# A hybrid layer of selective scan, attention and spectral filters: tokens laid over the partitions in blocks of 128 neighbours

## The chip, the cores and the metric

The kernel runs on one core of a Trainium2 chip. The metric is device time in microseconds (us) of a whole execution, as the median of several runs. Below, TensorE is called PE, VectorE DVE, ScalarE ACT, GpSimd POOL, and SyncE, which issues the transfers, SP, as the profile calls them.

## The reference

The input is 4 images (batches) of 48 x 48 positions, that is 2304 tokens, with 128 channels in float32. Two layers follow each other. Cut to what matters here:

```
# layer 0: selective scan (256 inner channels, 16 states, 4 directions)
xz = gn(x) @ in_proj_w.T;  xin, z = split(xz)
xc = silu(depthwise_conv3x3(xin));  y = sum of 4 directional scans of xc
y  = layernorm(y) * silu(z);        x = x + y @ out_proj_w.T
# layer 1: attention without projections, then STU
t = tokens(x)
n = ln(t);  t = t + softmax(n @ n.T) @ n          # 2304 x 2304 a batch
u = ln(t)
t = t + STU(u)   # causal convolutions of u with 16 filters, and a 3-tap
                 # autoregression; four weightings over 1, 1/2, 1/4, 1/8 of the tokens
```

All arithmetic of the kernel is float32.

## The kernel before

A batch goes through four pieces of work. The **prologue** normalizes the image, projects it and convolves it. The **scans** run the four directions in chunks of 384 tokens: ACT makes exponentials, DVE runs the recurrences (L461), POOL and PE sum over the states. The **epilogue** normalizes the sum of the scans, gates it, projects it to 128 channels and adds it to the residual. **Attention** follows, and its `tail` ends it. Then comes **STU**. Work of different batches is laid over one another: STU of batch b runs beside the scans of batch b+1, on PE above all, and the prologue of batch b+1 is handed out, task by task, between the steps of the epilogue and of the attention of batch b. After the last batch, STU runs alone.

The schedule is written out by hand: each engine executes its instructions in the order in which the program issues them, and the generators (`next(at)`, `parts.pop(0)()`) set that order. So an engine that waits holds up all that was issued to it later. DMAs are issued by SP alone in this part of the kernel, in order too, and SP itself waits where a transfer needs another one to have landed.

The 2304 tokens are cut into five pieces: `PIECES = [4, 4, 4, 4, 2]`, in blocks of 128 tokens, so four pieces J of 512 tokens and a last one of 256. The residual of the batch is held in SBUF as `T`, 128 partitions x 18 columns of 128 channels; piece J takes the columns 4J to 4J + n. Which token lies where is told by one function, `tokens(x, J)`, used for the load of `T` (L613) and for the store of the attention's result to the DRAM tensor `td` (L874):

```python
return x[512 * J:512 * J + P * n].rearrange("(p j) c -> p j c", j=n)
```

Partition p thus holds n neighbouring tokens, 2 KB in one stretch for n = 4. STU wants the tokens split into four phases, token modulo four, and with n = 4 the columns of `T` are those phases. The last piece has n = 2, and for it alone `tail` reads `td` back into a tile `tu` in four phases (L880).

The epilogue works channel-major: `yf` (the tensor `ya`) and `zr` hold channels on the partitions and tokens along the free axis. Its output must be token-major, so they are the stationary operand of the projection `op` (L654), and `sq` is that of the variance `var` (L639); the 128 tokens of column j are taken with a stride of n:

```python
nc.tensor.matmul(var[:, 4 * J + j:4 * J + j + 1], sq[J][:, 0, j:P * n:n], dmean[:, 0:1], ...)
nc.tensor.matmul(p[:, i, f], x[h][:, lo:lo + P * n - j0 - f:n], w[:, h], ...)
```

The stages of the epilogue are staggered over the pieces. One step (slot) issues, oldest piece first: the normalization for attention (`norm`), `add(J,2)` (L663, L665: DVE adds the projection, scaled by `rd`, to `T`), `project(J,2)` with `add(J,0)`, then for the next piece `project(J,0)` with `variance(J)` (its `rd`: DVE L642, POOL L643), for the next `gate` (DVE L633, POOL L634), then `center` (DVE L626, ACT L627) and `means` (PE L619). The two PSUM buffers of `op` alternate, so a projection waits for the `add` of the one two before it. Between these stages stand the prologue's tasks (transposes L195 with the copy L199 and the statistics L200).

Attention takes the pieces of queries in the order 0, 4, 1, 2, 3, each in 18 slots: scores `s` (L718), exponential `e` (ACT, L720), values `o` (L711). The tail of a finished piece is handed out one step a slot during the next piece: transposes `otr`, `add` to `T` (L871, L872), the store `td`, the normalization (`normed`: `ln_su` L149, L151, ACT `usq` L152, L154, POOL L156, L158), transposes `utr` (L890), copy `uT` (L893) and store `ud` (L895). The tail of piece 3 has no slots left and is issued at a stretch; after it come the first instructions of the next stage: STU's `prime` (L970) and its loads `tt<-fd` (L953) on SP, and the scans of the next batch.

Of the kernel before, what the change touches and what calls it, by code (L numbers as in the profile page):

```python
# [8 lines left out]
F32 = mybir.dt.float32  # L9
# [6 lines left out]
P = 128  # L16
B, H, W, C = 4, 48, 48, 128
# [38 lines left out]
def hybrid_kernel(ctx: ExitStack, tc: tile.TileContext, a: dict, out: bass.AP):  # L56
# [3 lines left out]
    nc = tc.nc  # L60
# [51 lines left out]
    dmean = wp.tile([P, P], F32, name="dmean")  # L112
# [20 lines left out]
    td = res.tile([L, C], F32, name="td")  # L133
# [6 lines left out]
    def tokens(x, J):  # L140

        n = PIECES[J]
        return x[512 * J:512 * J + P * n].rearrange("(p j) c -> p j c", j=n)

    def normed(x, d, eps, small, sq, name):

# [448 lines left out]
    def epilogue(b, T, xn, xnT, tmp, pool, ps):  # L595

        yf = [t.rearrange("p h w -> p (h w)") for t in yaccs.pop(b)]
        zr, mu, o, sq, rd, lns, pt = {}, {}, {}, {}, {}, {}, {}
        var = ps.one.tile([P, 512], F32, tag="var", name=f"var{b}")

        def at(J):
            return slice(512 * J, 512 * J + P * PIECES[J])

        def load_z(J):
            n = P * PIECES[J]  # L610
            zr[J] = tmp.tile([P, NH, 512], F32, tag=f"zr{J}", name=f"zr{b}_{J}")
            nc.sync.dma_start(zr[J][:, :, :n], zs[:, :, at(J)].rearrange("h p t -> p h t"))
            nc.sync.dma_start(T[:, 4 * J:4 * J + PIECES[J]], tokens(a["x"][b], J))  # L613

        def means(J):
            n = P * PIECES[J]
            mu[J] = ps.two.tile([P, 512], F32, tag="mu", name=f"mu{b}_{J}")
            for h in range(NH):
                nc.tensor.matmul(mu[J][:, :n], dmean, yf[h][:, at(J)], start=(h == 0), stop=(h == NH - 1))  # L619

        def center(J):
            n = P * PIECES[J]
            sq[J] = tmp.tile([P, NH, 512], F32, tag=f"esq{J % 3}", name=f"sq{b}_{J}")
            for h in range(NH):
                v = yf[h][:, at(J)]
                nc.vector.tensor_tensor(v, v, mu[J][:, :n], ALU.subtract)  # L626
                nc.scalar.activation(sq[J][:, h, :n], v, AF.Square)  # L627

        def gate(J):
            n = P * PIECES[J]  # L630
            for h in range(NH):
                v = yf[h][:, at(J)]
                nc.vector.tensor_tensor(v, v, zr[J][:, h, :n], ALU.mult)  # L633
            nc.gpsimd.tensor_tensor(sq[J][:, 0, :n], sq[J][:, 0, :n], sq[J][:, 1, :n], ALU.add)  # L634

        def variance(J):
            n = PIECES[J]
            for j in range(n):
                nc.tensor.matmul(var[:, 4 * J + j:4 * J + j + 1], sq[J][:, 0, j:P * n:n], dmean[:, 0:1],  # L639
                                 start=True, stop=True)  # L640
            rd[J] = tmp.tile([P, 4], F32, tag=f"rd{J}", name=f"rd{b}_{J}")[:, :n]
            nc.vector.tensor_scalar_add(rd[J], var[:, 4 * J:4 * J + n], 1e-5)  # L642
            nc.gpsimd.tensor_tensor(rd[J], rd[J], mhalf[:, :n], ALU.pow)  # L643

        def project(J, j0):
            n = PIECES[J]
            if j0 >= n:
                return
            o[J, j0] = p = ps.two.tile([P, 2, 2, C], F32, tag="o", name=f"op{b}_{J}_{j0}")
            for f in range(2):  # L650
                for i, (x, w) in enumerate(((yf, owg), ([zr[J][:, h] for h in range(NH)], owb))):
                    lo = 512 * J * (i == 0) + j0 + f
                    for h in range(NH):
                        nc.tensor.matmul(p[:, i, f], x[h][:, lo:lo + P * n - j0 - f:n], w[:, h],  # L654
                                         start=(h == 0), stop=(h == NH - 1))

        def add(J, j0):
            if j0 >= PIECES[J]:
                return
            p = o.pop((J, j0))  # L660
            for f in range(2):
                t = T[:, 4 * J + j0 + f]
                nc.vector.scalar_tensor_tensor(t, p[:, 0, f], rd[J][:, j0 + f:j0 + f + 1], t, ALU.mult, ALU.add)  # L663
            t = T[:, 4 * J + j0:4 * J + j0 + 2]
            nc.vector.tensor_tensor(t, t, p[:, 1], ALU.add)  # L665

        def norm(J):
            if J not in lns:
                n = PIECES[J]
                sq = pool.two.tile([P, 4, C], F32, tag="ln_sq", name=f"asq{b}_{J}")[:, :n]  # L670
                lns[J] = normed(T[:, 4 * J:4 * J + n], xn[:, 4 * J:4 * J + n], 1e-5, pool.two, sq, f"a{b}_{J}")
            next(lns[J], None)

        def turned(J):
            pt[J] = ps.two.tile([P, 512], F32, tag="tr", name=f"xtr{b}_{J}")
            for j in range(PIECES[J]):
                nc.tensor.transpose(pt[J][:, j * P:(j + 1) * P], xn[:, 4 * J + j], ident)

        def kept(J):
            nc.scalar.copy(xnT[:, at(J)], pt.pop(J)[:, :P * PIECES[J]])  # L680
            nc.gpsimd.memset(xn[:, 4 * J:4 * J + PIECES[J], C - 1:], 1.0)

        for J in range(len(PIECES)):
            load_z(J)
        stages = [means, center, gate, lambda J: (project(J, 0), variance(J)), lambda J: (project(J, 2), add(J, 0)),
                  lambda J: add(J, 2), norm, norm, norm, turned, kept]
        for slot in range(len(PIECES) + len(stages) - 1):
            for s, stage in reversed(list(enumerate(stages))):
                if 0 <= slot - s < len(PIECES):
                    stage(slot - s)  # L690
                    yield slot - s if stage is kept else None
# [158 lines left out]
    def tail(b, J, T, po, pool, ps):  # L850


        u, sums = us[b]
        n, k = PIECES[J], KP[J]
        T = T[:, 4 * J:4 * J + n]
        oT = pool.two.tile([P, 512], F32, tag="oT", name=f"oT{b}_{J}")
        nc.vector.tensor_copy(oT[:, :P * n], po[:, :P * n])
        yield
        p = ps.two.tile([P, 4, C], F32, tag="tr", name=f"otr{b}_{J}")[:, :n]
        for j in range(n):  # L860
            nc.tensor.transpose(p[:, j], oT[:, j * P:(j + 1) * P], ident)
        yield
        r, s = [pool.two.tile([P, 4], F32, tag=f"den{i}", name=f"den{i}_{b}_{J}")[:, :n] for i in range(2)]
        nc.vector.tensor_copy(r, p[:, :, C - 1])
        nc.vector.reciprocal(r, r)
        nc.vector.tensor_reduce(s, p[:, :, :C - 1], AX.X, ALU.add)
        nc.vector.tensor_tensor(s, s, r, ALU.mult)
        yield
        for j in range(n):
            t = T[:, j, :C - 1]  # L870
            nc.vector.scalar_tensor_tensor(t, p[:, j, :C - 1], r[:, j:j + 1], t, ALU.mult, ALU.add)  # L871
        nc.vector.tensor_tensor(T[:, :, C - 1], T[:, :, C - 1], s, ALU.subtract)  # L872
        yield
        nc.sync.dma_start(tokens(td, J), T)  # L874
        x = T
        if n < 4:

            yield
            x = pool.one.tile([P, 4, C], F32, tag="tu", name=f"tu{b}")
            nc.sync.dma_start(x[:k], td[512 * J:].rearrange("(p j) c -> p j c", j=4))  # L880
            for i in range(3):
                yield
        sq = pool.one.tile([P, 4, C], F32, tag="sq", name=f"usq{b}_{J}")
        for _ in normed(x[:k], u[:k, J], 1e-5, pool.two, sq, f"u{b}_{J}"):
            yield
        nc.vector.tensor_tensor(sums[:k, J], u[:k, J, 0:2], u[:k, J, 2:4], ALU.add)
        yield
        p = ps.two.tile([P, 512], F32, tag="tr", name=f"utr{b}_{J}")[:, :4 * k]
        for j in range(4):
            nc.tensor.transpose(p[:, j * k:(j + 1) * k], u[:k, J, j], ident[:k, :k])  # L890
        yield
        uT = pool.two.tile([P, 4 * P], F32, tag="uT", name=f"uT{b}_{J}")[:, :4 * k]
        nc.scalar.copy(uT, p)  # L893
        yield
        nc.sync.dma_start(ud[:, :, 1 + P * J:1 + P * J + k], uT.rearrange("c (j p) -> c j p", j=4))  # L895
# [255 lines left out]
    for b in range(B):  # L1151
# [14 lines left out]
        T = back.one.tile([P, NT, C], F32, tag="T", name=f"T{b}")  # L1166
# [93 lines left out]
```

## Time and profile before

| | |
|---|---|
| median of 3 runs | 6137.34 us (6124.15 to 6143.45) |
| the profiled execution, its own time | 6131.63 us |
| its span, first to last instruction | 6129.9 us |
| PE busy | 5042.3 us, 82% |
| DVE busy | 4264.0 us, 70% |
| POOL busy | 3630.6 us, 59% |
| ACT busy | 3258.1 us, 53% |
| DMA | 1062.79 MB, 173 GB/s over the span |
| PE L654 `op` (two halves, x288 each) | 79.1 and 76.2 us busy |
| PE L639 `var`, x144 | 32.9 us busy |
| SP L613 T<-in_x, SP L874 td<-T | 20 issues each |
| SP L880 tu<-td | 4 issues |

A busy time is summed over the span; the share is of the span. PE overlaps one instruction's end with the next one's start, so for a series the distance of two starts says more than the length of one. A matmul of the program appears as two PE instructions. The epilogue and attention of the four batches lie at about 1104 to 1394, 2466 to 2757, 3832 to 4121 and 5202 to 5438 us of the span. "Granted clock" is the share of full speed at which PE was allowed to run.

### The profile page before, as it was taken

To read this page: it belongs to the slowest core of one execution; us is meant where nothing else is said; L and a number is where in the kernel's file an instruction comes from. 1 tells how busy PE (TensorE), PEld (TensorE's weight loads), DVE (VectorE), ACT (ScalarE), POOL (GpSimd) and SP (SyncE) were. 2 spreads that over 40 slices of the span, in tenths; PEclk is the share of its full clock that TensorE was granted. 3 is DMA by queue.
4 is the path that set the end of the run, shared out by engine and by line. 5 is a ranking of instruction groups with operands and counts; after the bars stand their busy time and mean duration, and the time that the engine had idled before them with its cause. 6 is when DMAs were issued, how large, how long until landed. Compare 5 with 4: busy or idle time off the path is not lost.

```text
span 6129.9 us, 76036 instructions
## 1 busy us (share of the span) xinstructions
PE 5042.3 (82%) x24850; PEld 3316.1 (54%) x24850; DVE 4264.0 (70%) x4926; ACT 3258.1 (53%) x6909; POOL 3630.6 (59%) x1823
## 2 busy tenths in 40 slices
PE   3555555797889988788889988888889998889999
PEld 1111111445556667545556666535556666558889
DVE  6999999458888998458888898448889998210000
ACT  2666666246666665247666665247666665232111
POOL 1988889307788888207788888108778887100000
PEclk6777777799999999899999999889999999899999
DMA  3445444117767777117767777027777776035546
GB/s 109 157 147 165 156 157 159 33 65 205 215 209 244 234 248 250 38 65 223 210 216 238 234 245 247 30 79 220 210 222 236 233 251 228 7 87 156 159 141 208
DMA packets 734954, 1062.79 MB, mean 173 GB/s; under 512 B 158272, under 2 KB 543424, under 8 KB 734528
## 3 DMA queue, kind: packets, MB, share of 16 engines
q1 hardware_dynamic: 728736, 1054.63, 54.6%
q10 hardware_dynamic: 5824, 3.30, 0.3%
q8 instruction: 199, 3.26, 0.2%
q14 instruction: 195, 1.60, 0.1%
HBM read 939.60 MB, written 117.98 MB: 173 GB/s over the span
## 4 chain that ended last, share of the span: by engine, by line
PE 43%; DVE 25%; DMA 11%; ACT 10%; SPq 5%; issue 4%; POOL 2%; ACTq 0%; DVEq 0%; POOLq 0%
PE cx L992 13%; DVE s L461 12%; PE cy L992 6%; DVE s L451 6%; DMA rep<-dtdud 4%; PE s L718 4%; PE y L478 3%; PE o L711 3%; ACT dA L458 3%; SPq L430 3%; DMA bc<-xdd 3%; PE pr L1055 2%; DMA tt<-fd 2%; PE pr L1051 2%; PE op L654 2%
## 5 line engine op out<-in xcount | busy, mean ns | idle before, releaser
L461 DVE TENSOR_TENSOR_SCAN s<-dA,s 128x385 f32<-128x385 f32 x3072 | 2735.4, 942 | 496.5 <-ACT dA L458 494.2
L470 POOL TENSOR_TENSOR s<-s,bc 128x1536 f32<-128x1536 f32 x768 | 2440.1, 3178 | 171.7 <-DVE s L461 95.0
L458 ACT ACTIVATE dA<-rep,A 128x384 f32<-128x384 f32 x3072 | 1747.2, 584 | 504.0 <-DVE s L461 471.2
L451 POOL TENSOR_TENSOR s<-rep,bc 128x1536 f32<-128x1536 f32 x288 | 993.4, 3449 | 90.6 <-DMA bc<-xdd 90.6
L478 PE MATMUL y<-s,csum 128*32 128x384 f32 x6144 | 723.9, 546 | 239.7 <-DVE ya L484 154.6
L992 PE MATMUL cx<-tt,u 128*128 128x254 f32 (+7 forms) x3840 | 830.8, 361 | 83.6 <-DMA tt<-fd 49.2
L992 PE MATMUL cx<-tt,us 128*128 128x254 f32 (+7 forms) x3840 | 809.5, 353 | 52.3 <-ACT U L1012 24.9
L451 DVE TENSOR_TENSOR s<-rep,B 128x1536 f32<-128x1536 f32 x480 | 830.4, 1730 | 14.2 <-ACT B L443 14.2
L992 PEld LDWEIGHTS cx<-tt,u 128*128 128x128 f32 x3840 | 653.5, 197 | 279.9 <-issue 132.9
L992 PE MATMUL cy<-tt,u 128*128 128x252 f32 (+5 forms) x3840 | 787.1, 348 | 0.0
L992 PEld LDWEIGHTS cx<-tt,us 128*128 128x128 f32 x3840 | 641.2, 191 | 240.3 <-issue 82.8
L992 PEld LDWEIGHTS cy<-tt,u 128*128 128x128 f32 x3840 | 639.8, 190 | 146.2 <-issue 85.9
L1079 DVE TENSOR_TENSOR res<-res,ot 126x512 f32<-126x512 f32 (+1 forms) x20 | 13.4, 671 | 686.5 <-PE ot L1073 686.1
L478 PEld LDWEIGHTS y<-s,csum 128*32 128x32 f32 x6144 | 128.3, 112 | 589.8 <-issue 375.5
L469 POOL COPY carry<-s 128x4 f32<-128x4 f32 x640 | 121.6, 190 | 535.2 <-DVE s L461 523.5
L1011 ACT COPY U<-cx 128x252 f32<-128x252 f32 (+1 forms) x320 | 111.8, 349 | 597.3 <-PE cx L992 594.4
L834 PE MATMUL G<-M,W 128*128 128x256 f32 (+3 forms) x512 | 255.5, 620 | 174.6 <-DMA M<-in_M_phi_plus 92.7
L720 ACT ACTIVATE e<-s,shift 128x512 f32<-128x512 f32 (+1 forms) x360 | 231.1, 644 | 312.8 <-PE s L718 312.2
L718 PE MATMUL s<-xnT 128*128 128x512 f32 (+1 forms) x720 | 355.8, 579 | 42.9 <-ACT xnT L680 23.6
L156 POOL TENSOR_TENSOR ln_vu<-ln_vu,mhalf 128x4 f32<-128x4 f32 (+1 forms) x20 | 26.8, 1342 | 603.5 <-DVE ln_vu L155 603.5
L443 ACT COPY B<-bc 128x384 f32<-128x384 f32 x480 | 229.9, 479 | 251.8 <-DVE s L451 222.8
L1055 PEld LDWEIGHTS pr<-U,G 128*128 128x128 f32 x2048 | 304.4, 191 | 102.8 <-issue 78.6
(165 smaller groups left out, 4951.7 us busy)
## 6 DMA issues: line engine op xcount, KB each, us to landing
rep<-dtdud SPq DMA_DIRECT2D x768, 384.0 KB, 5.2
bc<-xdd SPq DMA_DIRECT2D x3072, 48.0 KB, 3.2
tt<-fd SPq DMA_DIRECT2D x192, 577.0 KB, 4.2
tt<-fd SPq DMA_DIRECT2D x192, 505.0 KB, 4.4
dtdud<-re SPq DMA_DIRECT2D x192, 384.0 KB, 4.2
tt<-fd SPq DMA_DIRECT2D x192, 379.0 KB, 3.5
G<-gd SPq DMA_DIRECT2D x192, 256.0 KB, 5.4
tt<-fd SPq DMA_DIRECT2D x64, 506.0 KB, 5.5
```

Source lines behind the costliest of these rows:

```text
L430: nc.sync.dma_start(t[c::C4], src[row].partition_broadcast(DL))
L443: nc.scalar.copy(self.bt[:, :CS], self.ch.bc[self.q])
L451: eng.tensor_tensor(s, self.ch.rep[self.h][:, :, 1], bt.unsqueeze(1).to_broadcast([P, G4, CS]), ALU.mult)
L458: nc.scalar.activation(dA[:, 1:CS + 1], ch.rep[self.h][:, g, 0], AF.Exp, scale=A[:, ch.k, self.h * G4 + g, self.q:self.q + 1])
L461: nc.vector.tensor_tensor_scan(s, dA[:, CS + 1:0:-1] if ch.rev else dA[:, :CS + 1], s, 0.0, ALU.mult, ALU.add)
L470: nc.gpsimd.tensor_tensor(self.s, self.s, ch.bc[Q4 + self.q].unsqueeze(1).to_broadcast([P, G4, CS]), ALU.mult)
L478: nc.tensor.matmul(ch.y[g * DL:(g + 1) * DL, :CS], csum, self.s[:, g], start=(self.q == 0), stop=(self.q == Q4 - 1))
L718: nc.tensor.matmul(p[:, :w], xnT[:, i * P:(i + 1) * P], xnT[:, 512 * J:512 * J + w], start=True, stop=True)
L720: nc.scalar.activation(e[:, :w], p[:, :w], AF.Exp, bias=shift)
L834: nc.tensor.matmul(p[:, :n], W[:, q if t else 0, i], M[t][:, i].unsqueeze(1).to_broadcast([P, n, C]), start=(t == 0 and i == 0), stop=(t = ...
L992: nc.tensor.matmul(p4[:, 2 * g:2 * g + 2, v - (hi - at):], x, t[:, :, hi - 1 - at + J * P:end if end >= 0 else None:-1], start=(c == 0 and ...
L1055: nc.tensor.matmul(p[:, 1 - g, :, v0:v1], G, U[n][:, ::-1 if g else 1, g, 1, v0:v1], start=False, stop=(k == KF - 1 and g == 1 and v1 == w))
```

## The change

A piece's tokens are laid out differently: column j of piece J holds the 128 neighbours from token 512J + 128j on, one a partition, for all pieces. The stationary operands of `var` and `op` become 128 consecutive columns. Loads and stores through `tokens` keep their count and bytes, and each partition's part is now n stretches of 512 B, not one of n x 512 B. The columns of `T` are no longer STU's phases, so `tail` reads `td` back into `tu`, four phases a partition, for every piece: a load and four further steps in each tail that had none. The attention itself sees the keys and queries in another order, the same for both.

```diff
 def tokens(x, J):
     n = PIECES[J]
-    return x[512 * J:512 * J + P * n].rearrange("(p j) c -> p j c", j=n)
+    return x[512 * J:512 * J + P * n].rearrange("(j p) c -> p j c", j=n)
...
 def variance(J):
     n = PIECES[J]
     for j in range(n):
-        nc.tensor.matmul(var[:, 4 * J + j:4 * J + j + 1], sq[J][:, 0, j:P * n:n], dmean[:, 0:1],
+        nc.tensor.matmul(var[:, 4 * J + j:4 * J + j + 1], sq[J][:, 0, j * P:(j + 1) * P], dmean[:, 0:1],
                          start=True, stop=True)
...
 def project(J, j0):
...
-            lo = 512 * J * (i == 0) + j0 + f
+            lo = 512 * J * (i == 0) + (j0 + f) * P
             for h in range(NH):
-                nc.tensor.matmul(p[:, i, f], x[h][:, lo:lo + P * n - j0 - f:n], w[:, h],
+                nc.tensor.matmul(p[:, i, f], x[h][:, lo:lo + P], w[:, h],
                                  start=(h == 0), stop=(h == NH - 1))
...
 def tail(b, J, T, po, pool, ps):
...
     nc.sync.dma_start(tokens(td, J), T)
-    x = T
-    if n < 4:
-
+    yield
+    x = pool.one.tile([P, 4, C], F32, tag="tu", name=f"tu{b}_{J}")
+    nc.sync.dma_start(x[:k], td[512 * J:512 * J + 4 * k].rearrange("(p j) c -> p j c", j=4))
+    for i in range(3):
         yield
-        x = pool.one.tile([P, 4, C], F32, tag="tu", name=f"tu{b}")
-        nc.sync.dma_start(x[:k], td[512 * J:].rearrange("(p j) c -> p j c", j=4))
-        for i in range(3):
-            yield
     sq = pool.one.tile([P, 4, C], F32, tag="sq", name=f"usq{b}_{J}")
     for _ in normed(x[:k], u[:k, J], 1e-5, pool.two, sq, f"u{b}_{J}"):
```

## The prediction

> **What bounds the kernel now.** I read the page first: four near-equal batches, each a long scan stage (VectorE's L461 first in the groups) and a short stage of epilogue and attention, in which the DMA row falls to 1 tenth. All that changes lies in those four short stages, so I read the chain of waits from 1060 to 1450 us next.
>
> ```profile
> 1120.39 7.46 PE op L654 x32
> 1127.85 1.77 PE var L639 x8
> 1130.79 2.34 DVE ya L633 x2
> 1133.13 1.20 DVE ya L626 x2
> 1135.45 7.71 PE op L654 x32
> 1143.15 1.77 PE var L639 x8
> ```
>
> The epilogue is a strict alternation: TensorE projects (op) and forms variances (var), VectorE waits for var, then gates, centres and adds, and its add frees the PSUM buffer that the next op needs. What TensorE does is not hidden. VectorE's timeline says it from the other side:
>
> ```profile
> 1129.65 0.16 DVE L642 TENSOR_SCALAR rd<-var 128x4 f32<-128x4 f32 x1 [7.12 <-PE var L639]
> 1144.95 0.16 DVE L642 TENSOR_SCALAR rd<-var 128x4 f32<-128x4 f32 x1 [7.62 <-PE var L639]
> 1160.13 0.16 DVE L642 TENSOR_SCALAR rd<-var 128x4 f32<-128x4 f32 x1 [8.61 <-PE var L639]
> ```
>
> The bracket is idle time and what ended it; over the run VectorE waits 135.6 us in 20 such places, the ceiling of what faster projections can return. Now the pace of the projections, from TensorE's timeline at two places:
>
> ```profile
> 1155.37 1.10 PE L654 MATMUL op<-owb,zr 128*128 128x128 f32 x4
> 1156.30 1.10 PE L654 MATMUL op<-owg,ya 128*128 128x128 f32 x4
> ...
> 1170.00 1.06 PE L654 MATMUL op<-owg,ya 128*128 128x128 f32 x4
> 1170.85 0.74 PE L654 MATMUL op<-owb,zr 128*128 128x128 f32 x4
> 1171.43 0.64 PE L654 MATMUL op<-owg,ya 128*128 128x128 f32 x4
> 1171.90 0.64 PE L654 MATMUL op<-owb,zr 128*128 128x128 f32 x4
> 1172.38 0.53 PE L639 MATMUL var<-dmean,sq 128*128 128x1 f32 x4
> ```
>
> Start to start is what counts (a reference matmul is two instructions). In pieces of four blocks, whose stationary operand takes every fourth float, four instructions take 0.93 us, 0.2333 each. In the last piece (every second float) they take 0.47, 0.1187 each. Same instruction, same shape: the difference is the stride. At 1170.00 four still take 0.85, 0.2125 each: there the granted clock was 0.50 (windows of 1 us), against 1.00 at 1172. The pieces of four run at 0.2333 at either clock. For var the paces are 0.222 (1.77 for eight) and 0.0975 (from 1172.38 to TensorE's next start at 1172.77).
>
> The other end of the stage: the last piece's read-back as it exists today (piece 4, last batch), and the final tail, which has none:
>
> ```profile
> 5337.93 0.32 SPq L874 DMA_DIRECT2D td<-T  x1
> 5339.67 0.48 SPq L880 DMA_DIRECT2D tu<-td  x1
> 5342.11 0.68 DVE L149 TENSOR_REDUCE ln_su<-tu 64x4 f32<-64x512 f32 x1 [4.21 <-DMA tu<-td]
> ...
> 5431.77 0.33 SPq L874 DMA_DIRECT2D td<-T  x1
> 5431.77 0.69 DVE L149 TENSOR_REDUCE ln_su<-T 128x4 f32<-128x512 f32 x1
> 5437.00 1.09 PE L890 MATMUL utr<-ident,u 128*128 128x128 f32 x4 [7.55 <-DVE u L158]
> ```
>
> With the read-back, 4.2 us lie between the store's issue and the reduction; without it, none. In the final tail VectorE, ScalarE, GpSimd and TensorE all stand behind this chain.
>
> **What the Trainium skill says.** "SBUF — State Buffer", Door 1: The DMA port swizzle, describes 16-byte lines in SBUF: a stride is free as long as two accesses fall into a line. Four floats are 16 bytes, one hit per line; two floats give two. The trace agrees: 0.2333 against 0.1187 us. "TensorE: Matmul & The Clock Gate", Part 1, says that TensorE starts at half clock after idleness and is released after about 3.4 us of activity in a free-running window; the 1 us windows here show 0.50 and 1.00, with release 3.1 to 6.3 us after a burst begins. "DMA: Bandwidth & Descriptors", Specifications, puts line rate at 512 B or more, so the new pieces of 512 B should not collapse; x<-in_x, already of that size, lands in 3.0 us for 192 KB. Its section on the anatomy of one DMA gives about 2.0 us fixed (for GpSimd's path); here store and load together took 4.2.
>
> **Part 1, the stride leaves L654 and L639.** It concerns the four pieces of four; the last goes from stride 2 to 1, taken as nothing. Five steps of a batch:
> - First (16 op, 8 var, clock 1.00): 16 x 0.1146 + 8 x 0.125 = 2.8 us.
> - Second (32 op, 8 var, clock 1.00): 3.67 + 1.0 = 4.7; but the second half of op waits for add(J,0), which VectorE reaches some 2.3 us after the first half may start, and the first half now takes 1.9: less 0.4, 4.2 (rounded down).
> - Third and fourth: they begin at clock 0.50 after idleness. Release in the eight such bursts came after 4.8, 3.4, 3.1, 4.8, 4.9, 3.4, 3.5 and 6.3 us, mean 4.3. Before: 0.27 of start + 32 x 0.2333 + 8 x 0.222 = 9.5. After: 0.27 + 19 at 0.2125, 13 at 0.1187, 0.8 for var = 6.6. 2.9 each, 5.8.
> - Fifth (16 op at 0.50, then the last piece): 16 x 0.0208 = 0.3.
>
> Sum 13.1 a batch, 52 in four; less 1 for a stretch at 0.50 in the second batch (2482 to 2485): **-51 us**. Ends: 36 (release always at 6.3 us) to 66 (clock always 1.00 in the first four steps, some 16.5 each). VectorE's wait at L642 is 4.4 to 8.6 us in these steps, so it absorbs every saving without becoming the bound; GpSimd's pow (1.0 to 1.4) and the add of sq (1.3 to 1.7) follow L642 as before and precede the next var by several us.
>
> **Part 2, 512 B pieces in T<-in_x and td<-T.** Same issues, bytes and order on SP. The first T is issued at 1077 and first used at 1121; those issued at 1098 to 1100 are used from 1150 on. Cover 30 us or more, cost nothing; without cover each would cost under 1 us (the 3.0 us row against a load of like size).
>
> **Part 3, sixteen new loads tu<-td, and four slots more in each of those tails.** Each load waits on SP for its store to land; behind it on SP stand zd<-z, xdd, dtdud, rep and bc issues in the middle of the stage, and ud<-uT and tt<-fd at its end.
> - The final tail of each batch (piece 3): everything is behind it, nothing covers. 4.2 us is the existing row at 128 KB; this store and load are 256 KB each and the store is cut into 512 B. I take 5.0 (4.2 to 6.5): 4 x 5.0 = **+20 us**.
> - Piece 0 in the last batch: its slots are short (0.86 us, 256 columns), four of them are 3.4 against 5.0 for the round trip; ScalarE's square and the transposes wait longer, with exp queued behind: **+2**.
> - The other eleven: four slots of 1.72 us or more are 6.9 and cover 5.0. In batches with a prologue VectorE has convolutions of 2.6 us (L262) between; there ScalarE's square already holds up exp (TensorE idle 5.2 us at 1315), and moving it four slots on may cost or return some. Unknown, from -12 to +12; I take 0.
>
> **Sum** -51 + 20 + 2 = **-29 us** on the profiled execution's own 6131.63 (span 6129.9): 6103. That run is 5.7 below the median of the three shown, 6137.34, from which it would be 6108. I give **6106**.
>
> **Rivals.**
> - *Every read-back is exposed.* One mechanism: VectorE takes ln_su in order, so if the store and load outlast the slots, it stalls, and ScalarE's square holds exp and so TensorE. 16 x 5 = 80 against 51: +29, **6161, slower**. It decides from ten exposed read-backs on. For it: the existing tu load still leaves VectorE waiting 10.2 us in 4. Against: those waits stand in slack (TensorE runs on without a gap at 5342).
> - *The clock takes the gain.* Shorter bursts never get released; 160 instructions x 0.0208 = 3.3 a batch, -13 + 22: +9, **6141**. Against: even at half clock a burst of 32 op lasts 6.8 us, beyond the longest release seen, 6.3.
> - *The stride was not the cause* and op stays at 0.2333: +22, **6154**. Against: the last piece's 0.1187.
>
> **How the numbers follow.** Main case 0.80, with its own range 6084 to 6125; exposed 0.07; clock 0.10; stride 0.03. A measurement here can tell about 0.3%, 18 us, from no change. Nine tenths of the main case are beyond it: faster 0.72; the rest of it with the clock case, and a little of the others: same 0.19; slower 0.09. The range 6084 to 6136 takes in the main case, and the better end of the clock case.
>
> **What would show it.** Right: op of all pieces at about 0.12 (clock 1.00) or 0.21 (0.50) start to start; VectorE's wait for var from 135.6 to some 85 us; five steps of an epilogue some 48 us instead of 61; twenty tu loads; in each final tail about 5 us between td<-T and ln_su. Wrong: op still 0.23, the clock at 0.50 through whole bursts, or gaps of several us in TensorE's attention before utr in most pieces.

## The result, and the profile after

The changed kernel takes 6108.49 us (median of 4 runs, 6095.52 to 6115.06) against 6138.39 (4 runs) beside it: 0.9952 of the time before, 95% interval 0.9929 to 0.9976. A second measurement of the same two kernels gave 0.9956 (0.9944 to 0.9969). It is faster by some 27 to 30 us; 29 with a forecast of 6106 had been predicted. The profiled execution took 6095.52 us, the fastest of the four, so its own move (36 us) is larger than the median's.

First the chain of waits of the changed kernel, in the stretch shown of before. The columns are start, length, and what the chain went through.

```profile
1119.55 2.02 PE op L654 x16
1121.57 0.80 PE var L639 x8
...
1123.53 2.34 DVE ya L633 x2
1125.88 1.20 DVE ya L626 x2
...
1128.19 6.31 PE op L654 x32
1134.50 0.80 PE var L639 x8
```

The alternation of TensorE and VectorE is the same, and so are VectorE's pieces (2.34 and 1.20). Only TensorE's became shorter: var 1.77 to 0.80, the 32 op 7.71 to 6.31 where the granted clock is 0.50 for most of the burst, 7.46 to about 4.4 where it is 1.00. TensorE's timeline of the second step shows the latter, with the short wait that the prediction had set at 0.4:

```profile
1117.11 0.61 PE L654 MATMUL op<-owg,ya 128*128 128x128 f32 x4
1117.55 0.61 PE L654 MATMUL op<-owb,zr 128*128 128x128 f32 x4
1118.00 0.61 PE L654 MATMUL op<-owg,ya 128*128 128x128 f32 x4
1118.44 0.61 PE L654 MATMUL op<-owb,zr 128*128 128x128 f32 x4
1119.55 0.68 PE L654 MATMUL op<-owg,ya 128*128 128x128 f32 x4 [0.49 <-DVE T L665]
```

Four instructions take 0.447 us start to start, 0.112 each instead of 0.233. In VectorE's timeline, the waits for var shrink by what TensorE gave back:

```profile
1122.39 0.16 DVE L642 TENSOR_SCALAR rd<-var 128x4 f32<-128x4 f32 x1 [2.99 <-PE var L639]
1135.32 0.16 DVE L642 TENSOR_SCALAR rd<-var 128x4 f32<-128x4 f32 x1 [5.25 <-PE var L639]
1148.53 0.16 DVE L642 TENSOR_SCALAR rd<-var 128x4 f32<-128x4 f32 x1 [6.65 <-PE var L639]
```

Over the run that wait is 83.4 us, from 135.6. The other end of the stage, in the timeline of the last batch's final tail, has got its read-back:

```profile
5389.65 0.36 SPq L874 DMA_DIRECT2D td<-T  x1
5391.97 0.33 SPq L877 DMA_DIRECT2D tu<-td  x1
5394.57 0.69 DVE L149 TENSOR_REDUCE ln_su<-tu 128x4 f32<-128x512 f32 x1 [4.95 <-DMA tu<-td]
5399.79 1.09 PE L887 MATMUL utr<-ident,u 128*128 128x128 f32 x4 [12.46 <-DVE u L158]
```

4.92 us from the store's issue to the reduction, where there had been none, and TensorE's wait grows from 7.55 to 12.46. Cutting each batch at four events that exist in both traces tells the whole move of the profiled execution:

| summed over four batches, us | before | after | move |
|---|---|---|---|
| first op to first score of attention | 288.5 | 236.1 | -52.4 |
| to the issue of td<-T of piece 3 | 747.1 | 746.5 | -0.6 |
| to the transposes utr of piece 3 | 30.6 | 50.2 | +19.7 |
| everything else (scans, STU, start) | 5063.7 | 5061.0 | -2.7 |
| span | 6129.9 | 6093.8 | -36.1 |

That "everything else" hardly moved is in part chance: in the single profiled executions of all kernels below it lies between 5061 and 5082 us. So the moves of the three stretches say more than the difference of two spans.

### The profile page after: what moved, and what is told of

Same layout as the page of the kernel before. It is cut to its first block, busy times and chain, and to the rows that moved or that the text cites. A ratio compares the mean times of both kernels' runs of the same rounds, so it can differ in the third digit from the quotient of the medians.

```text
span 6093.8 us, 76036 instructions
## 1 busy us (share of the span) xinstructions
PE 4984.4 (82%) x24850; PEld 3260.2 (54%) x24850; DVE 4263.5 (70%) x4926; ACT 3257.2 (53%) x6909; POOL 3625.5 (59%) x1823
## 4 chain that ended last, share of the span: by engine, by line
PE 42%; DVE 25%; DMA 13%; ACT 9%; SPq 5%; issue 4%; POOL 2%; ACTq 0%; POOLq 0%; DVEq 0%
PE cx L989 13%; DVE s L461 11%; PE cy L989 7%; DVE s L451 5%; DMA rep<-dtdud 4%; PE s L718 4%; PE o L711 3%; PE y L478 3%; ACT dA L458 3%; DMA tt<-fd 3%; SPq L430 3%; PE pr L1052 2%; DMA bc<-xdd 2%; DVE xc L262 2%; PE pr L1048 2%
## 5 line engine op out<-in xcount | busy, mean ns | idle before, releaser
L156 POOL TENSOR_TENSOR ln_vu<-ln_vu,mhalf 128x4 f32<-128x4 f32 (+1 forms) x20 | 21.8, 1092 | 627.1 <-DVE ln_vu L155 627.1
```

## Experiments

The theory: two independent moves, -52 from the stride of the stationary operand, +20 from the round trip through DRAM in each final tail. The rivals: the gain comes from elsewhere; all read-backs cost; the 512 B pieces make the round trip long. Ratios are against the kernel before, measured on the same chip: its median was 6134.87 beside the layout alone, the read-back alone, the changed kernel and turning on the chip; 6139.72 beside the old layout of piece 3 and the other strides; 6132.17 beside turning in pairs.

### The layout alone

The edit is to the changed kernel.

```diff
-        yield
-        x = pool.one.tile([P, 4, C], F32, tag="tu", name=f"tu{b}_{J}")
-        nc.sync.dma_start(x[:k], td[512 * J:512 * J + 4 * k]...)
-        for i in range(3):
-            yield
+        x = T
+        if n < 4:
+            ... (the read-back of the last piece, as before)
```

> The change without its new read-backs: columns of 128 neighbours, but only the last piece is read back in four phases, so STU gets the tokens of the other pieces in a wrong order (that part is not the reference's). Theory (the stride of 16 bytes was the price, the read-back of piece 3 is the cost): the epilogue's gain alone, about -52 us, ratio 0.9915; the wait of VectorE for var falls to some 83 us as in the changed kernel, and td<-T is followed by ln_su at once in the final tail. Rival (the gain comes from something else in the changed tail or from where the stages fall): it stays near the changed kernel's ratio, 0.995.

Measured: 0.9916 (0.9901 to 0.9931), median 6087.12. In the profiled execution, first op to first score takes 237.0 us in four batches, and VectorE waits 84.1 us for var. (That execution, 6100.10 us, was the slowest of the five: everything else took 5082.0 us in it, 18 more than in the profile of before.) In its last tail the reduction follows the store at once:

```profile
5398.42 0.36 SPq L874 DMA_DIRECT2D td<-T  x1
5398.43 0.69 DVE L149 TENSOR_REDUCE ln_su<-T 128x4 f32<-128x512 f32 x1
5403.65 1.09 PE L890 MATMUL utr<-ident,u 128*128 128x128 f32 x4 [7.55 <-DVE u L158]
```

The gain is that of the new layout, it lies in the stretch of the projections, and it is the larger half of two.

### The read-back alone

The edit is to the kernel before.

```diff
-        x = T
-        if n < 4:
-            yield
-            ...
+        yield
+        x = pool.one.tile([P, 4, C], F32, tag="tu", name=f"tu{b}_{J}")
+        nc.sync.dma_start(x[:k], td[512 * J:512 * J + 4 * k].rearrange("(p j) c -> p j c", j=4))
+        for i in range(3):
+            yield
```

> The kernel before with the read-back of all five pieces, and the old layout (2 KB pieces, stride 4 in op and var). Theory: only the final tail of each batch is exposed, some 4.5 to 5 us each, and piece 0 of the last batch 2 to 3: +20 to +23 us, ratio 1.0035. Rival 1, every read-back is exposed: +80 us, ratio 1.013. Rival 2, the 512 B pieces make the round trip long: then ln_su follows the store here after 4.2 us or less, against 4.9 in the changed kernel, and the ratio is 1.003.

Measured: 1.0036 (1.0023 to 1.0048), +22 us. Its last tail:

```profile
5446.90 0.32 SPq L874 DMA_DIRECT2D td<-T  x1
5448.94 0.32 SPq L877 DMA_DIRECT2D tu<-td  x1
5451.51 0.69 DVE L149 TENSOR_REDUCE ln_su<-tu 128x4 f32<-128x512 f32 x1 [4.63 <-DMA tu<-td]
```

4.61 us with stores of 2 KB pieces against 4.92 with 512 B, and all four final tails of each kernel agree with these within 0.05: the small pieces cost 0.3 us a round trip, about 1 us in the four final tails, so rival 2 has the sign and not the size. Rival 1 asked for 1.013 and falls. In the profile, issue of td<-T to utr of piece 3 takes 49.0 us in four batches, 18.4 more than before, and everything else takes 5063.6, as before (5063.7): what the final tail loses, the later work does not give back, and the ratio agrees. The two halves sum to -29.5 by their ratios (-51.5 and +22); the changed kernel in the same comparison moved by -27:

> The changed kernel once more, beside the others on one chip: ratio 0.9952 as before (0.993 to 0.998), between the two halves: the sum of the moves of layout_only and readback_only within 8 us.

Measured: 0.9956 (0.9944 to 0.9969), median 6104.57.

### Only piece 3 in the old layout

The edit is to the changed kernel, written short.

```diff
-        return x[512 * J:...].rearrange("(j p) c -> p j c", j=n)
+        return x[512 * J:...].rearrange("(p j) c -> p j c" if J == 3 else "(j p) c -> p j c", j=n)
...
+        cols = slice(lo + j0 + f, lo + P * n, n) if J == 3 else slice(lo + (j0 + f) * P, ...)
...
-        (read-back of every piece)
+        (read-back of every piece but piece 3)
```

> The changed kernel with piece 3 alone in the old layout (stride 4 in its op and var, no read-back). Theory: the exposed round trip of the final tail goes, 4 x 4.9 = 20 us back; the strided projections of one piece of four return, 2 to 3 us a batch, 8 to 12 in all. So 8 to 12 us below the changed kernel, about -40 us, ratio 0.9935. Rival (the final tail's wait was hidden by what the scans then wait for anyway): as the changed kernel or above it, 0.995 to 0.997.

Measured: 0.9930 (0.9918 to 0.9942), median 6098.47. Its final tails have no wait for `tu`: issue of td<-T to utr of piece 3 takes 30.6 us in four batches, from 50.2 in the changed kernel, and first op to first score takes 245.9 us, 9.8 more than in the changed kernel: 20 given back for 10 taken, as expected. By the ratios the gain over the changed kernel is larger, some 13 to 16 us, but these were taken on two chips. That the final tail's wait was on the path is shown by this kernel and by the read-back alone.

### Other strides

Every second float, with two neighbours a partition (`"(i p j) c -> p i j c", j=2`; op and var read `lo:lo + 2 * P - f:2`):

> The changed kernel with columns at a stride of two floats: two neighbours a partition (1 KB pieces), op and var read every second float. By lines of 16 bytes a stride of two is free: op at 0.11 to 0.12 us start to start at full clock, 0.213 at half, VectorE's wait for var about 83 us. Rival (a stride costs in proportion): about 0.16 to 0.17 at full clock.

Every third float in the kernel before (`m = 3`; op reads `lo:lo + P * m - m + 1:m`):

> The kernel before with every third float in place of every fourth in op and var of the pieces of four (the columns taken are not those of the reference; the count of instructions and their shapes stay). If each new line of 16 bytes costs a fixed time, three lines for four reads: about 0.175 us start to start. If only a stride of 16 bytes or more is slow: 0.12. If two hits a line are needed: 0.233.

TensorE's timelines, at full clock, of the kernel with every second float and then of that with every third:

```profile
1114.01 0.63 PE L654 MATMUL op<-owg,ya 128*128 128x128 f32 x4
1114.48 0.63 PE L654 MATMUL op<-owb,zr 128*128 128x128 f32 x4
```

```profile
1113.31 0.86 PE L655 MATMUL op<-owg,ya 128*128 128x128 f32 x4
1114.00 0.86 PE L655 MATMUL op<-owb,zr 128*128 128x128 f32 x4
1114.70 0.86 PE L655 MATMUL op<-owg,ya 128*128 128x128 f32 x4
```

Start to start of one instruction in us, from the timelines of the kernels with each stride:

| stride in floats | granted clock 1.00 | granted clock 0.50 |
|---|---|---|
| 1 | 0.112 | 0.213 |
| 2 | 0.118 | 0.213 |
| 3 | 0.174 | 0.213 |
| 4 | 0.233 | 0.233 |

So it is not a threshold: a stride of 3 lies between. Nor is a stride of 2 priced midway, as the rival had it. Every entry is the longer of two times: one that follows the clock (0.112 or 0.213) and one of 0.058 us for each float of stride, which at a stride of 4 is the same at both clocks. Up to a stride of four floats the lines of 16 bytes that 128 columns touch are 32 for each float of stride (96 at 3, 128 at 4), so this is also 1.8 ns a line. The runs can't tell a price for lines from one for distance: a stride of eight floats, with the lines of four and twice the distance, would, and was not run. In the Trainium skill, "SBUF — State Buffer" (Door 1: The DMA port swizzle) has the lines of 16 bytes and calls for two hits a line for full bandwidth; the trace agrees in that two hits (0.118) are nearly free, and a stride of 3, with 1.33 hits, lies between one and two. VectorE's wait for var with every second float was 88.6 us where about 83 had been expected; where the 5 us come from was not looked into. One run each, 6109.44 and 6113.42, of which only the paces are used; with every third float the columns are not those of the reference.

### Turning on the chip, and in pairs

The old layout and the old tail stay; the epilogue turns the tokens itself. (Written short: `by` stands for the rearrangement of the operand.)

```diff
+            yp[J] = tmp.tile(...); zp[J] = tmp.tile(...)
-                nc.vector.tensor_tensor(v, v, mu[J][:, :n], ALU.subtract)
-                nc.scalar.activation(sq[J][:, h, :n], v, AF.Square)
+                nc.vector.tensor_tensor(yp[J] by "p (j q) -> p q j", v by "p (q j) -> p q j", mu[J] likewise, ALU.subtract)
+                nc.scalar.activation(sq[J][:, h, :n], yp[J][:, h, :n], AF.Square)
+                nc.scalar.copy(zp[J] by "p (j q) -> p q j", zr[J] by "p (q j) -> p q j")
... (gate, var and op work on yp and zp, op and var with contiguous columns)
```

> Another way to contiguous columns: the old layout of the tokens and the old tail stay, and in the epilogue VectorE's centering writes, and a copy on ScalarE of zr writes, their results in four phases into new tiles, so that op and var read 128 neighbours. If writing at a stride of 16 bytes costs VectorE nothing and ScalarE's four extra copies a piece stay beside: the gain without the cost, -52 us, ratio 0.9915. If the strided write doubles VectorE's centering (0.65 us an instruction, two a step, twenty steps, in the chain): -26, ratio 0.9958.

Measured: 0.9968 (0.9956 to 0.9979), a gain of 20 us (13 to 27): the first case is excluded, and the second, -26, is just within. Its groups of 512 floats (count, then busy us, mean ns of one, idle us before):

```profile
L634 ACT COPY zp<-zr 128x512 f32<-128x512 f32 x32 | 31.6, 1086 | 0.0
L627 DVE TENSOR_TENSOR yp<-ya,mu 128x512 f32<-128x512 f32 x32 | 30.9, 1043 | 9.0 <-PE mu L619 9.0
L643 DVE TENSOR_TENSOR yp<-yp,zp 128x512 f32<-128x512 f32 x32 | 28.4, 909 | 10.6 <-ACT zp L634 10.6
```

Centering takes 1043 ns, from 678. The expectation speaks of a stride of 16 bytes; in the kernel each write jumps 512 bytes, to the next block of 128, so that 512 floats are 512 writes, each to another line than the one before: 2.0 ns a write. The last pieces, of 256 floats, take 602 ns in VectorE and 638 in ScalarE's copy, so 256 writes more cost 441 and 448 ns, 1.7 to 1.8 ns each. Over all forty, those of the last pieces with them, centering is busy 11.7 us more (35.1, from 23.4), and the copies, 1086 ns each, make the gate wait 10.6 us in all, which the estimate had left out. These two leave about 30 of the 52 us; why no more than 20 were measured was not followed further. If changes of line are what costs, then moving pairs halves them:

```diff
-            yp by "p (j q) -> p q j"
+            yp by "p (a q b) -> p q a b", b=2      # zp likewise
-            op and var read lo:lo + P
+            op and var read lo:lo + 2 * P - f:2
-        stages = [means, lambda J: (center(J), turn_z(J)), gate, ...]
+        stages = [lambda J: (means(J), turn_z(J)), center, gate, ...]
```

(`yp` takes the buffers of `zr` whose copy is done, so that all fits.)

> As turn_on_chip, but centering on VectorE and the copy of zr on ScalarE write in pairs: two neighbours stay side by side, so a write makes two of four bytes' steps before it jumps, and op and var read every second float; the copy of zr stands one step earlier. If what a write or a read costs is the number of 16-byte lines that it touches (about 1.8 ns a line, 256 lines here against 512), both are hidden below the engines' own pace: centering at 0.68 us (1.04 in turn_on_chip), the copy near 0.63 (1.09), op at 0.119; the epilogue then gains nearly what layout_only gained, with no read-back: -44 to -50 us, ratio 0.992 to 0.993. If any step that is not contiguous costs them, centering stays at 1.0 and the ratio at 0.996 to 0.997.

Measured: 0.9908 (0.9891 to 0.9924), median 6079.91, somewhat better than expected. Its interval lies wholly below the changed kernel's (on another chip) and overlaps that of the layout alone. The same groups:

```profile
L643 DVE TENSOR_TENSOR yp<-yp,zp 128x512 f32<-128x512 f32 x32 | 23.8, 784 | 0.4
L626 DVE TENSOR_TENSOR yp<-ya,mu 128x512 f32<-128x512 f32 x32 | 20.4, 679 | 8.4 <-PE mu L619 8.4
L634 ACT COPY zp<-zr 128x512 f32<-128x512 f32 x32 | 19.1, 649 | 13.3 <-DMA zr<-zd 13.2
```

Centering is back at 679 ns, the copy at 649, and the gate waits no more for it: that is 2.5 to 2.7 ns for each pair, above the 1.7 to 1.8 that a write to another line cost, so the jumps no longer show. First op to first score takes 237.9 us, within 1 us of the layout alone, and no piece of four is read back. The earlier place of the copy and the pairs were changed together, so how the gate's 10.6 us divide between them stays open; the fall of the two durations is put to the pairs, since centering is back at what its contiguous writes took (678).

## Why the prediction was right

- **What bounds the stage.** The reading that VectorE and TensorE alternate without overlap carried the sum: TensorE's saving, 52.4 us in the profiled executions, equals VectorE's lost waiting, 135.6 - 83.4 = 52.2.
- **Part 1, -51.** Measured -52.4 in the traces, -51.5 by the ratio of the layout alone. By starts of op, over four batches: first steps 12.3 us (predicted 11.2), second 16.7 (16.8), third and fourth together 21.8 (23.2), fifth to the last var 1.6 (1.3). The 1 us taken off for the second batch was not lost: its stretch moved by 13.1, like the others. The single third and fourth steps scatter, from 2.0 to 3.4 against 2.9 predicted, with the release of the clock: 12 to 27 of their 32 op ran at half pace, on average 19 to 20, where 19 had been set. So the mean of 4.3 us held, and no single step was to be foreseen: in each of the two traces all 277 changes of the granted clock fall on a grid of 3.41 us (in the kernel before at 1130.15, 1140.39, 1143.80, 1154.04, 1160.87 and 1171.11), and each burst starts at another place in it. Taking the last piece's step from stride 2 to 1 as nothing was nearly right (0.118 to 0.112).
- **Part 2, nothing.** The loads of T showed no wait; the stores cost the 0.3 us a round trip above, which had been put within Part 3.
- **Part 3, +22.** Final tails 19.7 us for 20. Piece 0 of the last batch: +2.9 for 2. From the first score to the store of piece 3 that batch went from 157.4 to 160.3 us, and all of it lies in the queries of pieces 0 and 4 (57.4 to 60.3), where the tail of piece 0 is handed out. The other three batches moved by -3.4 in that stretch, where 0 within 12 had been set; but this zero is a balance, not the cover that the prediction gave as its reason. The queries of pieces 0 and 4 took about 1 us more in each of these batches, those of piece 2 some 2.5 less. In the first batch these fell from 45.1 to 42.3 (42.5 in the read-back alone, 44.9 in the layout alone): there the normalization of piece 1 now comes four slots later, and ScalarE's wait before its square falls from 7.5 to 0.7 us. The prediction had named such a return as possible and left its size open. And "four slots of 1.72 us or more are 6.9 and cover 5.0" does not hold for VectorE. In the last batch, without a prologue, it waits 4.4 to 5.1 us for `tu` in every tail, and longest for piece 2 beside a prologue, 9.65 us, where the load takes 6.5 us to be usable:

```profile
1334.71 0.37 SPq L874 DMA_DIRECT2D td<-T  x1
1337.87 0.54 SPq L877 DMA_DIRECT2D tu<-td  x1
1344.34 0.69 DVE L149 TENSOR_REDUCE ln_su<-tu 128x4 f32<-128x512 f32 x1 [9.65 <-DMA tu<-td]
```

 VectorE's waits for `tu` came to 73.1 us in the run, of which 19.8 are the final tails'. The rest cost little because TensorE carries that stretch (it runs on without a gap from 1334 to 1345), not because the slots cover the transfer. Why this load is the slow one was not tried; on SP four loads `rep` of 384 KB stand between its store and it, and four more follow.
- **Rivals.** All read-backs exposed (6161) and the stride not the cause (6154) are excluded by the two halves. The clock did take part of the gain in the steps that begin at 0.50, but not all: in the first batch op ran at 0.213 for 5.2, 6.1 and 2.8 us of the last three bursts and at 0.112 after it.

## What to carry to other kernels

Look at how often an operand's access moves to another line of 16 bytes, on TensorE's stationary side as well as in what VectorE and ScalarE write; at two floats a line it was nearly free here, and a permutation can be split in two halves, one in the writer and one in the reader, so that neither jumps for every float. A layout that is changed to feed one engine is paid where the old layout had been used for nothing: count that at the end of the stage, where no other work is left to cover a round trip. And a wait of an engine is worth its length only where that engine carries the stage.

## What was not expected of the hardware

- VectorE and ScalarE pay for scattered writes at nearly TensorE's rate for its stationary operand: 1.7 to 1.8 ns for each further write to another line (1043 and 1086 ns for 512), hidden in pairs (679 and 649).
- At a stride of four floats TensorE loses nothing by the half clock: 0.233 us at either. What the change wins, it wins at the full clock, and only 0.02 us an instruction at half.
- TensorE drops to half clock while it is executing: in the kernel before, at 1143.80 us of the span, in the middle of a burst begun at 1135, with TensorE busy throughout. Of the 3.41 us up to this point on the grid, the last 0.65 were var, whose moving operand is one column wide; 3.41 us of op alone, from 1154.04, were not followed by a drop. That var is the cause was not tested.
